# Another start for a four-layer graph network: the first graph's x before the weights, and the weight products shared out among three engines

## The chip, the cores and the metric

One Trainium2 chip, one of its cores. The metric is the device time of one execution in microseconds (us), the median over the runs. The engines are named as in the profile: PE is TensorE (matrix products), PEld its weight loads, DVE is VectorE, ACT is ScalarE, POOL is GpSimd, SP is SyncE, which here only issues DMAs. A "q" behind an engine's name is its instruction queue.

## The reference

128 independent graphs of 128 nodes with 512 features each, float32, pass four layers. Each layer is followed by `x = layernorm(x + layer(x))`.

```python
# layer 0, W1 = W2 = adj, so C - A is only the bias b
out = max over n of relu((adj @ x) + b)            # one number per node, added to its row
# layer 1: attention over the masked graph
h = x @ W;  s1 = h @ a[:512];  s2 = h @ a[512:]
e = leaky_relu(s1[:, None] + s2[None, :], 0.2) * adj
out = elu(softmax(e) @ h + beta * h)
# layer 2
out = (adj @ x) @ weight + bias
# layer 3: 8 heads of 64
q, k, v = x @ Wq + bq, x @ Wk + bk, x @ Wv + bv
out = softmax(q k^T / 8 + where(adj == 0, -1e9, 0)) v
```

## The kernel before

**Layer 1 without h.** The kernel never forms `h @ a`. It folds W into a once: `wa1 = W @ a[:512]` and `wa2 = W @ a[512:]`, two vectors of 512, each spread over all 128 partitions (`wa_bc[0]` and `wa_bc[1]`). After that s1 and s2 of a graph are row sums of `x1 * wa_bc[i]` (line 440). To build `wa_bc`, `w1_a` multiplies the four chunks of W (128x512 each) with a half of a that a DMA has spread over the partitions (`a_bc`), sums each row on the way (line 319, four instructions on DVE for each half), lays the four columns of sums on a diagonal (`wa_diag`, line 322) and lets a product with a matrix of ones spread them (line 333); line 336 copies the result out of PSUM.

**A graph's steps.** `l0` is layer 0: a product with adj^T (line 424, `psA`), its row maximum (line 427, `mx`), relu with the bias (line 431, `rl`), adding it to x (line 432), then the layer norm. Every layer norm is four engines' work: statistics on DVE (377, 379), three instructions of 128x1 on POOL (382, 384, 386: `ve`, `rstd`, `nmr`), the normalising pass on ACT (388). Then come the attention of layer 1 (`e`, `pe`, `att`), `zT` = (att x)^T, `z` = the product with W, `yT` and `y` for layer 2, `xT` (x3 turned), and for each group of four graphs q, k and v of layer 3, `sc` (scores) and `av` (weights times v).

**Sevens.** All big products but those of the first four graphs use a scheme with seven products of half-size blocks in place of eight. It needs sums and differences of blocks: of the weights, once (`weight_sums`, line 367, four instructions of 128x512 for each of the five weight matrices), and of the data, each time (`T`, line 732, four for each group; `Tz` and `Ty`, line 550). The first four graphs ("early") take `z` and `y` as whole products, and turn by TensorE instead of by DMA.

**What sets the order.** The schedule is written out by hand: all instructions stand in each engine's queue in the order in which the Python code emits them, and every engine works through its queue in order, waiting in front of each instruction until its inputs are there. The class `Plan` decides that order. It keeps an estimated clock for each engine; a step is a Python generator that yields `(engine, us, landing, rank)` before it emits, and resumes when the estimate says that the engine is free. `place` gives the TensorE steps their priorities, buffers are counted in `plan.left`, and `mark` says that something is ready. So an altered cost or mark at the beginning can alter the emitted order anywhere behind it.

**Loads.** SP's queue: adj, the two halves of `a` (each read from HBM once for each of 128 partitions, 256 KB), then x of graph 0 and graph 1, then x of each later graph when one of the two `x0` buffers is free, that is after the last use in line 440 of the graph two before. ACT's queue: W1 in four pieces, then `later_loads`: W2, Wq, Wk, the bias of layer 2, Wv, the bias of v, at times that the plan sets.

Of the kernel before, what the change touches and what calls it, by code (L numbers as in the profile page):

```python
# [9 lines left out]
F32 = mybir.dt.float32  # L10
AF = mybir.ActivationFunctionType
ALU = mybir.AluOpType
AX = mybir.AxisListType

P = 128
# [132 lines left out]
def kernel(  # L148
# [18 lines left out]
    nc = tc.nc  # L167
    ctx.enter_context(tc.manual_schedule())
    B, N, C = x.shape
    NCC = C // P  # L170
    H, HD = 8, 64
# [6 lines left out]
    sb_bufs = {  # L178
# [4 lines left out]
    }  # L183
# [9 lines left out]
    small = ctx.enter_context(tc.tile_pool(name="small", bufs=5))  # L193
    plan = Plan({**sb_bufs, **ps_bufs, **hbm_bufs, "va": NV, "w": 0})

    def ps_tile(tag, name):
        return psum.tile([P, 512], F32, tag=tag, name=name, bufs=ps_bufs[tag])

    def sb_tile(tag, shape, name):
        return sb.tile(shape, F32, tag=tag, name=name, bufs=sb_bufs[tag])  # L200

    def get(tag, shape, name):
        yield tag
        return sb_tile(tag, shape, name)
# [5 lines left out]
    def dve(us, rank=1):  # L210
        return ("DVE", us - 0.09, 0.09, rank)

    def act(us, rank=1):
        return ("ACT", us - 0.1, 0.1, rank)

    def pool(us, rank=1):
        return ("POOL", us, 0.0, rank)

    def sp(us, landing, rank=1):
        return ("SP", us, landing, rank)  # L220
# [5 lines left out]

    def load_x(b):
        x0[b] = yield from get("x0", [P, C], f"x0_{b}")
        yield sp(0.35, 2.5 if b > 1 else 5.5 + b)
        nc.sync.dma_start(out=x0[b], in_=x[b])  # L230
        plan.mark(("x0", b))

# [13 lines left out]
        nc.gpsimd.dma_start(out=t, in_=v.rearrange("(c p) -> p c", p=P))  # L246
        return t

    a_flat = a1.rearrange("f o -> (f o)")
    a_bc = [None, None]  # L250
    for i in (1, 0):
        a_bc[i] = sb_tile("xp", [P, C], f"a_bc{i}")
        nc.sync.dma_start(out=a_bc[i], in_=a_flat[i * C : (i + 1) * C].partition_broadcast(P))
        plan.left["xp"] -= 1
    w1_sb, w1_in = load_w(w1, "w1_sb")
    for c in range(NCC):
        nc.scalar.dma_start(out=w1_sb[:, c], in_=w1_in[:, c])
# [11 lines left out]

    def later_loads():  # L270

        for us, dst, src in (
            (9.5, w2_sb, w2_in), (1.0, wq_sb, wq_in), (4.0, wk_sb, wk_in), (1.0, bias2_bc, bias2_in), (4.0, wv_sb, wv_in),
            (1.0, bv_bc, bv_in),
        ):
            yield sp(0.0, us)
            if len(src.shape) < 4:
                yield act(0.16)
                nc.scalar.dma_start(out=dst, in_=src)
                continue  # L280
            yield act(0.34)
            for b in range(NQ):
                nc.scalar.dma_start(out=dst[b * Q : (b + 1) * Q], in_=src[b])
# [23 lines left out]
    wa_bc = [const.tile([P, C], F32, tag=f"wa_bc{i}", name=f"wa_bc{i}") for i in range(2)]  # L307
    plan.engine["DVE"] = 6.0

    def w1_a():  # L310

        yield sp(0.0, 6.5)
        for i in (1, 0):
            junk = yield from get("x2", [P, C], f"wa_junk{i}")
            dg = yield from get("oT", [P, NCC, P], f"wa_diag{i}")
            yield dve(3.9)
            cols = small.tile([P, NCC], F32, tag="cols", bufs=2, name=f"wa_cols{i}")
            for c in range(NCC):
                nc.vector.scalar_tensor_tensor(
                    junk, w1_sb[:, c, :], 1.0, a_bc[i], ALU.mult, ALU.mult, accum_out=cols[:, c : c + 1]  # L320
                )
            nc.vector.tensor_tensor(
                dg,
                ident.unsqueeze(1).to_broadcast([P, NCC, P]),
                cols.unsqueeze(2).to_broadcast([P, NCC, P]),
                ALU.mult,
            )
            plan.give("x2")
            plan.give("xp")
            yield "mm"  # L330
            ps = ps_tile("mm", f"ps_wa{i}")
            yield ("PE", 1.0, 0.0, 1)
            nc.tensor.matmul(ps, ones, dg.rearrange("p c n -> p (c n)"), start=True, stop=True)
            plan.give("oT")
            yield dve(0.7)
            nc.vector.tensor_copy(wa_bc[i], ps)
            plan.give("mm")
            plan.mark(("wa", i))
        yield dve(0.5)
        nc.vector.tensor_scalar(bq_s, bq_col, QS, None, ALU.mult)  # L340
        nc.vector.tensor_scalar(beta_id, ident, beta_col, None, ALU.mult)
        plan.mark("beta_id")
# [5 lines left out]
    def weight_sums(n, w):  # L348

        t = const.tile([P, 3, 2, HALF], F32, tag=f"sums_{n}", name=f"sums_{n}")  # L350
        a11, a12, a21, a22 = (w[:, 2 * c : 2 * c + 2, r * HALF : (r + 1) * HALF] for r in range(2) for c in range(2))
        sums[n] = (a11, a12, a21, a22, t[:, 0], t[:, 1], t[:, 2])
        yield sp(0.0, {"z": 0.0, "y": 0.0, "q": 44.0, "k": 52.0, "v": 84.0}[n])
        if n == "q":
            for c in range(NCC):
                yield act(0.6)
                nc.scalar.mul(w[:, c, :], w[:, c, :], QS)
        if n in "zy":
            yield ("mark", ("whole", n))
        for dst, x_, y_, op in (  # L360
            (t[:, 0], a21, a22, ALU.add),
            (t[:, 1], t[:, 0], a11, ALU.subtract),
            (a21, a11, a21, ALU.subtract),
            (t[:, 2], a12, t[:, 1], ALU.subtract),
        ):
            yield pool(1.3)
            nc.gpsimd.tensor_tensor(dst, x_, y_, op)
            yield sp(0.0, 0.7)
        plan.mark(("sums", n))


# [47 lines left out]
    def l0(b):  # L419
        s = st[b]  # L420
        x1 = sb_tile("x1", [P, C], f"x1_{b}")
        xin_b = x0.pop(b)
        ps = ps_tile("mm", f"psA_{b}")
        nc.tensor.matmul(ps, adjT, xin_b, start=True, stop=True)  # L424
        yield dve(0.69)
        mx = small.tile([P, 1], F32, tag="mx0", bufs=3, name=f"mx0_{b}")
        nc.vector.tensor_reduce(mx, ps, AX.X, ALU.max)
        plan.give("mm")
        yield act(0.95)
        rl = small.tile([P, 1], F32, tag="rl", bufs=3, name=f"rl_{b}")  # L430
        nc.scalar.activation(rl, mx, AF.Relu, bias=b0_col)
        nc.scalar.activation(xin_b, xin_b, AF.Identity, bias=rl)  # L432
        yield from layernorm(xin_b, x1, f"0_{b}")
        s["x1"] = x1
        cols = []
        for i in (1, 0):
            yield ("mark", ("wa", i))
            yield dve(0.82)
            col = small.tile([P, 1], F32, tag=f"s{i}", bufs=6, name=f"s{i}_{b}")
            nc.vector.scalar_tensor_tensor(  # L440
                xin_b, x1, 1.0, wa_bc[i], ALU.mult, ALU.mult, accum_out=col
            )
            if i == 0:
                plan.give("x0")
                if b + sb_bufs["x0"] < B:
                    plan.at(plan.end, load_x(b + sb_bufs["x0"]))
            cols.append(col)
            if i and b < EARLY:
                dg = yield from get("s2_bc", [P, P], f"diag_{b}")
                yield dve(0.3)  # L450
                nc.vector.tensor_scalar(dg, ident, col, None, ALU.mult)
                s["diag"] = dg
                plan.mark(("diag", b))
        s2, s["s1"] = cols
        if b < EARLY:
            plan.mark(("s1", b))
            return
        s2_row = yield from get("s2_row", [P, Q], f"s2_row_{b}")
        yield dve(0.2)
        nc.vector.transpose(s2_row, s2.to_broadcast([P, Q]))  # L460
        d = yield from get_hbm("s2_hbm", [NQ, Q], f"s2_hbm_{b}")
        yield sp(0.35, 3.0)
        nc.sync.dma_start(out=d, in_=s2_row.rearrange("(q r) c -> q r c", r=Q)[:, 0, :])
        plan.give("s2_row")
        s2_bc = yield from get("s2_bc", [P, P], f"s2_bc_{b}")
        yield sp(0.35, 5.0)
        nc.sync.dma_start(out=s2_bc, in_=d.rearrange("q c -> (q c)").partition_broadcast(P))
        plan.give("s2_hbm")
        yield from attention(b, s2_bc, "s2_bc")
# [746 lines left out]
    }  # L1216
    total = {name: B for name in steps}
    total.update(s2=EARLY, attT=EARLY, xT=EARLY, pT=LATE, z1=EARLY, y1=EARLY, z=7 * (B - EARLY) // 2, y=7 * (B - EARLY) // 2, avT=B - LATE, av=2 * LATE, **{n: 7 * (B // GB) for n in "qkv"})
    for b in range(sb_bufs["x0"]):
        plan.at(1.0, load_x(b))  # L1220
    plan.at(0.0, w1_a())
    plan.at(0.0, later_loads())
    for n, w in (("z", w1_sb), ("y", w2_sb), ("q", wq_sb), ("k", wk_sb), ("v", wv_sb)):
        plan.at(0.0, weight_sums(n, w))
# [32 lines left out]
```

## Time and profile before

| what | value |
|---|---|
| median of 3 runs | 2707.15 us (2698.55, 2707.15, 2709.77) |
| the profiled execution's own time | 2699.37 us |
| its span, first to last instruction | 2697.3 us |
| its mean granted TensorE clock | 0.994 |
| PE busy | 2601.1 us (96%) |
| DVE, POOL, ACT busy | 2246.2 (83%), 1822.0 (68%), 1795.9 us (67%) |
| DMA | 425.11 MB, mean 158 GB/s |

The busy shares are means over the whole span. The table of windows, the waits and the timeline, which the next part shows, tell where the 4% without TensorE work lie. In them "x4" counts instructions, the time in brackets is what the engine idled before the instruction, and "<-" names what it waited for. A float32 product shows as two matmul records. Durations come from this one execution.

### The profile page before, as it was taken

To read this page: it belongs to the slowest core of one execution; us is meant where nothing else is said; L and a number is where in the kernel's file an instruction comes from. 1 tells how busy PE (TensorE), PEld (TensorE's weight loads), DVE (VectorE), ACT (ScalarE), POOL (GpSimd) and SP (SyncE) were. 2 spreads that over 40 slices of the span, in tenths; PEclk is the share of its full clock that TensorE was granted. 3 is DMA by queue.
4 is the path that set the end of the run, shared out by engine and by line. 5 is a ranking of instruction groups with operands and counts; after the bars stand their busy time and mean duration, and the time that the engine had idled before them with its cause. 6 is when DMAs were issued, how large, how long until landed. Compare 5 with 4: busy or idle time off the path is not lost. (4 is left out here: it accounts for less than half of the span.)

```text
span 2697.3 us, 48358 instructions
## 1 busy us (share of the span) xinstructions
PE 2601.1 (96%) x15393; PEld 2207.8 (82%) x15393; DVE 2246.2 (83%) x4561; ACT 1795.9 (67%) x4847; POOL 1822.0 (68%) x2664
## 2 busy tenths in 40 slices
PE   6899999999999999999999999999999999999998
PEld 3688878888888888888888888888888888888887
DVE  7579888888888888888888888888888898889876
ACT  4566667566666676666766767676767666667655
POOL 4756667766777667667667676667776667677665
PEclk8999999999999999999999999999999999999999
DMA  5145445555444555545565445654545644455553
GB/s 132 37 122 167 149 149 163 161 187 161 155 154 147 183 164 181 152 144 167 161 186 160 150 141 192 200 165 153 155 154 170 202 148 138 149 172 174 164 176 122
DMA packets 435006, 425.11 MB, mean 158 GB/s; under 512 B 99264, under 2 KB 319552, under 8 KB 434752
## 3 DMA queue, kind: packets, MB, share of 16 engines
q1 hardware_dynamic: 431504, 416.26, 49.7%
q10 hardware_dynamic: 3120, 5.77, 0.8%
q8 instruction: 122, 2.00, 0.3%
q14 instruction: 132, 1.08, 0.1%
q0 software_dynamic: 128, 0.01, 0.0%
HBM read 218.17 MB, written 203.75 MB: 156 GB/s over the span
## 5 line engine op out<-in xcount | busy, mean ns | idle before, releaser
L388 ACT ACTIVATE x<-x,nmr,rstd 128x512 f32<-128x512 f32 x384 | 311.2, 812 | 178.1 <-POOL nmr L386 170.9
L1045 ACT ACTIVATE pr<-pr,nm 128x128 f32<-128x128 f32 x992 | 386.2, 395 | 31.1 <-DVE nm L1040 30.1
L382 POOL TENSOR_SCALAR ve<-mv 128x1 f32<-128x1 f32 x512 | 137.9, 269 | 323.7 <-DVE mv L379 250.0
L384 POOL TENSOR_TENSOR rstd<-ve,nhalf 128x1 f32<-128x1 f32 x512 | 309.8, 605 | 42.6
L377 DVE BATCH_NORM_STATS2 stats<-x 128x6 f32<-128x512 f32 x384 | 259.7, 676 | 25.7 <-ACT x L432 24.7
L440 DVE SCALAR_TENSOR_TENSOR x<-x,wa_bc 128x512 f32<-128x512 f32 x256 | 218.0, 856 | 27.3 <-ACT x L388 26.6
L922 POOL TENSOR_TENSOR st_v<-st_v,bv_bc 128x512 f32<-128x512 f32 x96 | 124.5, 1297 | 138.8 <-ACT st_v L908 137.3
L706 POOL TENSOR_TENSOR x<-x,bias_bc 128x512 f32<-128x512 f32 x128 | 173.5, 1362 | 64.0 <-PE ps_yT L713 41.5
L1128 POOL TENSOR_TENSOR x3r<-turn_o,x3r 128x512 f32<-128x512 f32 x122 | 198.3, 1625 | 20.1 <-DMA x3r<-x_hbm 10.7
L1126 POOL TENSOR_TENSOR turn_o<-turn_o,rd 128x512 f32<-128x512 f32 x122 | 140.0, 1148 | 105.8 <-DVE turn_o L407 89.9
L386 POOL TENSOR_SCALAR nmr<-mv,rstd 128x1 f32<-128x1 f32 x512 | 160.7, 314 | 52.9
L1045 ACT ACTIVATION_READ_ACCUMULATOR pr<-pr,nm 128x1 f32 x976 | 188.7, 193 | 0.0
L407 DVE STREAM_TRANSPOSE turn_pr<-turn_pr 128x1024 f32<-128x1024 f32 x122 | 150.0, 1232 | 31.2 <-DMA turn_pr<-turn_hbm_pr 31.1
L1034 DVE TENSOR_TENSOR pr<-ps_sc,mask 128x512 f32<-128x512 f32 x248 | 162.0, 675 | 14.8 <-PE ps_sc L1012 14.5
L1114 ACT COPY oT<-ps_av 128x512 f32<-128x512 f32 x122 | 132.0, 1082 | 51.9 <-PE ps_av L1102 41.6
L411 DVE STREAM_TRANSPOSE xTh<-turn_x 128x512 f32<-128x512 f32 x124 | 137.5, 1112 | 15.1 <-DMA turn_x<-turn_hbm_x 14.3
L1040 DVE TENSOR_REDUCE nm<-pr 128x8 f32<-128x1024 f32 x124 | 147.7, 1202 | 2.2 <-ACT w_sb L1045 1.9
L559 PEld LDWEIGHTS ps_zT<-attT,x 128*128 128x128 f32 x1024 | 133.3, 192 | 19.4 <-issue 5.8
L424 PE MATMUL psA<-x,adjT 128*128 128x512 f32 x256 | 135.3, 614 | 10.6 <-DMA x<-in_x_dram 9.8
L1012 PEld LDWEIGHTS ps_sc<-kTh,qTh 64*128 64x128 f32 x2048 | 121.8, 187 | 27.1 <-issue 16.0
L388 ACT ACTIVATE x3r<-x3r,nmr,rstd 128x512 f32<-128x512 f32 x122 | 98.7, 812 | 65.9 <-POOL nmr L386 58.7
L559 PE MATMUL ps_zT<-attT,x 128*128 128x128 f32 x1024 | 137.7, 278 | 4.2 <-DVE attT L411 2.3
(198 smaller groups left out, 7666.4 us busy)
## 6 DMA issues: line engine op xcount, KB each, us to landing
turn_hbm_pr<-pr SPq DMA_DIRECT2D x122, 512.0 KB
turn_pr<-turn_hbm_pr SPq DMA_DIRECT2D x122, 512.0 KB
x<-in_x_dram SPq DMA_DIRECT2D x128, 256.0 KB
x3r<-x_hbm SPq DMA_DIRECT2D x128, 256.0 KB
x_hbm<-x SPq DMA_DIRECT2D x124, 256.0 KB
turn_hbm_x<-x SPq DMA_DIRECT2D x124, 256.0 KB
turn_x<-turn_hbm_x SPq DMA_DIRECT2D x124, 256.0 KB
turn_hbm_o<-oT SPq DMA_DIRECT2D x122, 256.0 KB
```

Of the source, the lines that this page charges most:

```text
L377: nc.vector.bn_stats(stats, src if flat is None else flat)
L384: nc.gpsimd.tensor_tensor(rstd, ve, nhalf, ALU.pow)
L386: nc.gpsimd.tensor_scalar(nmr, mv[:, 0:1], rstd, -1.0, ALU.mult, ALU.mult)
L388: nc.scalar.activation(dst, src, AF.Identity, bias=nmr, scale=rstd)
L407: nc.vector.transpose(t.rearrange("p a n c -> p (a n c)"), t.rearrange("p a n c -> p (a n c)"))
L440: nc.vector.scalar_tensor_tensor(xin_b, x1, 1.0, wa_bc[i], ALU.mult, ALU.mult, accum_out=col)
L559: nc.tensor.matmul(ps[:, c * P : (c + 1) * P], s["x1"][:, c * P : (c + 1) * P], attT, start=True, stop=True)
L706: nc.gpsimd.tensor_tensor(x2, x2, bias2_bc, ALU.add)
L1034: nc.vector.tensor_tensor(pr_h[:, NCC * e : NCC * (e + 1)], pss[e].rearrange("p f (b c) -> p f b c", b=NQ), mask_bc, ALU.add)
L1040: nc.vector.tensor_reduce(nm, pr_h, AX.XY, ALU.max, negate=True)
L1045: nc.scalar.activation(pr_h[:, i], pr_h[:, i], AF.Exp, bias=nm[:, i : i + 1], accum_out=None if late else den[:, i : i + 1])
L1128: nc.gpsimd.tensor_tensor(xp_m, o.rearrange("p a n c -> p a (n c)"), xp_m, ALU.add)
```

## The change

Seven edits, all in the first part of the program.

1. `a` is loaded once, as one row on one partition (`a_row`, 4 KB), instead of twice spread over 128 partitions.
2. x of graph 0 is issued on SP right behind it, by hand. The plan is told that it is there at 6.0; x of graph 1 is now what the plan's `load_x` starts with.
3. The row is spread by TensorE: two products with a row of ones into two PSUM banks (`a_bc`). ACT copies the first half to SBUF (`a_sb`); the second is read from PSUM.
4. `w1_a` is split. The products of W1 with the second half stay four instructions on DVE, one by one as W1's pieces come. Those with the first half become four multiplications on POOL, each followed by a pass on ACT that sums the rows. Both copies of line 336 go from DVE to ACT.
5. The load of W2 waits for `rl` of graph 0. Before, it was emitted straight behind W1.
6. The weight sums of q and k go from POOL to DVE, eight instructions of 128x512. Those of z, y and v stay on POOL.
7. In `weight_sums` the plan's pause of 0.7 behind each sum is taken out.

```diff
-        yield sp(0.35, 2.5 if b > 1 else 5.5 + b)
+        yield sp(0.35, 2.5 if b > 1 else 7.0)
...
-    for i in (1, 0):
-        a_bc[i] = sb_tile("xp", [P, C], f"a_bc{i}")
-        nc.sync.dma_start(out=a_bc[i], in_=a_flat[i * C : (i + 1) * C].partition_broadcast(P))
-        plan.left["xp"] -= 1
+    a_row = sb_tile("pr", [P, H * P], "a_row")[0:1, :]
+    nc.sync.dma_start(out=a_row, in_=a1.rearrange("f o -> o f"))
+    plan.left["pr"] -= 1
+    x0[0] = sb_tile("x0", [P, C], "x0_0")
+    nc.sync.dma_start(out=x0[0], in_=x[0])
+    plan.left["x0"] -= 1
+    plan.marks["x0", 0] = 6.0
...
+        yield ("mark", ("rl", 0))
         for us, dst, src in (
-            (9.5, w2_sb, w2_in), (1.0, wq_sb, wq_in), ...
+            (0.0, w2_sb, w2_in), (1.0, wq_sb, wq_in), ...
...
+    a_bc = [ps_tile("mm", f"ps_a{i}") for i in range(2)]
+    a_sb = sb_tile("x2", [P, C], "a_sb")
...
+    for i in range(2):
+        nc.tensor.matmul(a_bc[i], ones[0:1, :], a_row[:, i * C : (i + 1) * C], start=True, stop=True)
+    nc.scalar.copy(a_sb, a_bc[0])
+
+    def w1_a_part(i, c):
+
+        prod = yield from get("x2", [P, C], f"wa_prod{i}_{c}")
+        col = wa_cols[i][:, c : c + 1]
+        if i:
+            yield dve(0.82, 0)
+            nc.vector.scalar_tensor_tensor(prod, w1_sb[:, c, :], 1.0, a_bc[1], ALU.mult, ALU.mult, accum_out=col)
+        else:
+            yield pool(1.35, 0)
+            nc.gpsimd.tensor_tensor(prod, w1_sb[:, c, :], a_sb, ALU.mult)
+            yield act(0.95)
+            nc.scalar.activation(prod, prod, AF.Identity, accum_out=col)
...
     def w1_a(i):
...
-            yield dve(0.7)
-            nc.vector.tensor_copy(wa_bc[i], ps)
+        yield act(0.6)
+        nc.scalar.copy(wa_bc[i], ps)
...
-            yield pool(1.3)
-            nc.gpsimd.tensor_tensor(dst, x_, y_, op)
-            yield sp(0.0, 0.7)
+            if n in "qk":
+                yield dve(0.72, 2)
+                nc.vector.tensor_tensor(dst, x_, y_, op)
+            else:
+                yield pool(1.3)
+                nc.gpsimd.tensor_tensor(dst, x_, y_, op)
...
         nc.scalar.activation(rl, mx, AF.Relu, bias=b0_col)
+        if b == 0:
+            plan.mark(("rl", 0))
```

In the emitted programs PE has one product more for each half of `a`, ACT seven instructions more (a copy, four summing passes, two copies from DVE), POOL four fewer (four multiplications more, eight sums fewer), DVE two more (eight sums more, four products and two copies fewer), SP one DMA fewer. The two programs stand in different order on every engine to the end: of TensorE's 7,731 products, 4,088 stand in another place in a comparison of the two lists.

More of the change, by code (lines that the diff above doesn't have):

```diff
@@ L247, in load_col @@
         return t
-    a_flat = a1.rearrange("f o -> (f o)")
-    a_bc = [None, None]
-    for i in (1, 0):
-        a_bc[i] = sb_tile("xp", [P, C], f"a_bc{i}")
-        nc.sync.dma_start(out=a_bc[i], in_=a_flat[i * C : (i + 1) * C].partition_broadcast(P))
-        plan.left["xp"] -= 1
+    a_row = sb_tile("pr", [P, H * P], "a_row")[0:1, :]
[5 more added lines that the diff above has]
+    plan.marks["x0", 0] = 6.0
     w1_sb, w1_in = load_w(w1, "w1_sb")
@@ L270, in later_loads @@
     def later_loads():
+        yield ("mark", ("rl", 0))
         for us, dst, src in (
-            (9.5, w2_sb, w2_in), (1.0, wq_sb, wq_in), (4.0, wk_sb, wk_in), (1.0, bias2_bc, bias2_in), (4.0, wv_sb, wv_in),
+            (0.0, w2_sb, w2_in), (1.0, wq_sb, wq_in), (4.0, wk_sb, wk_in), (1.0, bias2_bc, bias2_in), (4.0, wv_sb, wv_in),
             (1.0, bv_bc, bv_in),
@@ L308 @@
     plan.engine["DVE"] = 6.0
[L310 to L327, printed above, removed]
-            plan.give("x2")
[L329 to L334, printed above, removed]
-            yield dve(0.7)
-            nc.vector.tensor_copy(wa_bc[i], ps)
-            plan.give("mm")
-            plan.mark(("wa", i))
@@ new lines @@
+    a_bc = [ps_tile("mm", f"ps_a{i}") for i in range(2)]
+    a_sb = sb_tile("x2", [P, C], "a_sb")
+    wa_cols = [small.tile([P, NCC], F32, tag="cols", bufs=2, name=f"wa_cols{i}") for i in range(2)]
+    plan.left["mm"] -= 2
+    plan.left["x2"] -= 1
+    for i in range(2):
[12 more added lines that the diff above has]
+            nc.scalar.activation(prod, prod, AF.Identity, accum_out=col)
+        plan.give("x2")
+        plan.mark(("col", i, c))
@@ new lines, in w1_a @@
+    def w1_a(i):
+        cols = wa_cols[i]
+        for c in range(NCC):
+            yield ("mark", ("col", i, c))
+        if i == 0:
+            plan.give("x2")
+            plan.give("pr")
+        plan.give("mm")
+        dg = yield from get("oT", [P, NCC, P], f"wa_diag{i}")
+        yield dve(0.75, 0)
+        nc.vector.tensor_tensor(
+            dg,
+            ident.unsqueeze(1).to_broadcast([P, NCC, P]),
+            cols.unsqueeze(2).to_broadcast([P, NCC, P]),
+            ALU.mult,
+        )
+        yield "mm"
+        ps = ps_tile("mm", f"ps_wa{i}")
+        yield ("PE", 1.0, 0.0, 1)
+        nc.tensor.matmul(ps, ones, dg.rearrange("p c n -> p (c n)"), start=True, stop=True)
+        plan.give("oT")
+        yield act(0.6)
+        nc.scalar.copy(wa_bc[i], ps)
+        plan.give("mm")
+        plan.mark(("wa", i))
+        if i:
+            return
@@ L1218 @@
     total.update(s2=EARLY, attT=EARLY, xT=EARLY, pT=LATE, z1=EARLY, y1=EARLY, z=7 * (B - EARLY) // 2, y=7 * (B - EARLY) // 2, avT=B - LATE, av=2 * LATE, **{n: 7 * (B // GB) for n in "qkv"})
-    for b in range(sb_bufs["x0"]):
+    for b in range(1, sb_bufs["x0"]):
         plan.at(1.0, load_x(b))
-    plan.at(0.0, w1_a())
+    plan.at(0.0, w1_a(1))
+    plan.at(0.0, w1_a(0))
+    for c in range(NCC):
+        for i in (1, 0):
+            plan.at(6.0 + 1.2 * c, w1_a_part(i, c))
     plan.at(0.0, later_loads())
```

## The prediction

> **What bounds the kernel now.** I first read the table of windows (columns: window, its length, then busy us and instruction count of PE, PEld, DVE, ACT and POOL, granted clock, DMA share, GB/s).
>
> ```profile
> 0.00:40.00 40.00, 20.36 (x48) 9.83 (x49) 25.89 (x68) 12.82 (x25) 9.32 (x22) 0.83 0.74 192
> 40.00:60.00 20.00, 17.62 (x69) 9.98 (x68) 17.44 (x38) 12.08 (x26) 13.24 (x20) 1.00 0.11 30
> 60.00:100.00 40.00, 29.03 (x120) 18.22 (x119) 23.91 (x55) 20.98 (x45) 34.34 (x44) 0.96 0.31 61
> 100.00:135.00 35.00, 33.69 (x163) 28.91 (x164) 20.95 (x44) 18.54 (x40) 22.50 (x28) 0.95 0.08 20
> 135.00:270.00 135.00, 134.88 (x776) 115.92 (x776) 111.06 (x237) 87.31 (x240) 82.16 (x123) 1.00 0.48 145
> 270.00:1350.00 1080.00, 1050.70 (x6265) 897.71 (x6262) 916.28 (x1868) 737.97 (x2006) 742.80 (x1094) 1.00 0.52 161
> 1350.00:2430.00 1080.00, 1061.53 (x6346) 906.34 (x6345) 927.69 (x1880) 740.48 (x2018) 749.51 (x1098) 1.00 0.53 164
> ```
>
> From 135 us on TensorE is the bound. Its idle time is 29.3 us in the first 1080 us behind 270 and 18.5 in the next. Before 135 it idles 40.00-20.36 = 19.6, then 2.4, 11.0 and 1.3: 34.3 us, and that is what an edit of the start can reach. Then I read the waits of PE up to 135 us (us in total, times, longest), and ACT's largest.
>
> ```profile
> PE psA L424 <- DMA x<-in_x_dram: 7.9, 2, 6.7
> PE ps_wa L333 <- DVE wa_diag L322: 5.1, 1, 5.1
> ...
> PE ps_q_chain L888 <- POOL T L732: 6.2, 1, 6.2
> PE ps_yT L713 <- ACT x L388: 3.2, 2, 1.7
> PE ps_y L600 <- ACT yT L540: 1.6, 1, 1.6
> ...
> ACT x L388 <- POOL nmr L386: 17.7, 9, 5.1
> ```
>
> Two chains, then: x and `wa_bc` for graphs 0 and 1, and later POOL, which has every layer norm and all weight sums in its queue (34.34 of 40 us busy from 60 to 100). Last, the timeline at these places.
>
> ```profile
> 10.74 3.75 PE L424 MATMUL psA<-x,adjT 128*128 128x512 f32 x4 [6.72 <-DMA x<-in_x_dram]
> 12.82 0.69 DVE L427 TENSOR_REDUCE mx<-psA 128x1 f32<-128x512 f32 x1 [0.45 <-PE psA L424]
> ...
> 20.56 2.08 PE L333 MATMUL ps_wa<-wa_diag,ones 128*128 128x512 f32 x2 [5.11 <-DVE wa_diag L322]
> ...
> 23.04 0.81 ACT L388 ACTIVATE x<-x,nmr,rstd 128x512 f32<-128x512 f32 x1 [3.02 <-POOL nmr L386]
> ...
> 27.44 2.08 PE L424 MATMUL psA<-x,adjT 128*128 128x512 f32 x2 [1.22 <-DMA x<-in_x_dram]
> ...
> 52.72 1.26 POOL L367 TENSOR_TENSOR sums_q<-wq_sb 128x512 f32<-128x512 f32 x1
> 52.80 1.73 DVE L440 SCALAR_TENSOR_TENSOR x<-x,wa_bc 128x512 f32<-128x512 f32 x1
> ...
> 100.22 3.51 PE L888 MATMUL ps_q_chain<-T,sums_q 128*128 128x256 f32 x8 [6.23 <-POOL T L732]
> ```
>
> A product of 512 columns takes 2.08 us behind idle time, 1.02 later. The chain that ended last lies in the last 12 us and says nothing on the start.
>
> **Loads (edits 1, 2, 5).** Up to 12 us the queues moved about 3.1 MB: adj, 0.5 MB of a, two x, W1 and W2. Without the spread a and W2 it is 1.6 MB; at the DMA view's rates in the first slices of 1.5 us (0, 187, 190, 249, 353, 330 GB/s) that is there at 8 us, not 12. So x of graph 0 comes between 5 and 8 us, not at 10.7, and W1's last piece at about 8, not 10.9. W2's megabyte then lies in front of Wq, Wk and Wv on ACT's queue: at the 230 GB/s of 20 to 30 us it pushes them back 4.4 us. Wq is first used at 47.3 (line 357), so I cost this at nothing; were it not covered, those 4.4 us would fall on the q sums. Costed the same way, at nothing: the issue of W2 (0.39), in front of the second `rl`.
>
> The one row has no counterpart; the nearest rows are adj (64 KB, issued 0.73, there at 3.57) and the bias of layer 0 (0.5 KB, 5.9 us to landing). Issued at 1.2, it lands between 4.0 and 7.1. I take 4.0, as adj goes by the same queue. The Trainium skill ("DMA: Bandwidth & Descriptors", rules for kernel authors) speaks against the edit: an access pattern whose outermost dimension is smaller than 16 confines a DMA to that many of the engines. By it the row would use one of 16; no run here shows what that costs for 4 KB.
>
> **Spreading a on TensorE (edit 3)** puts two cold products in front of the first `psA`: 2 x 2.08 from 4.0 to 8.2 us. So although x is there sooner, `psA` of graph 0 runs from 8.2 to 10.3, and its maximum is taken from 10.3, 2.5 us before 12.82. With the row at 7.1 all of this is 3.1 later: the gain is gone, and 0.6 lost.
>
> **wa_bc (edit 4).** DVE keeps four products of 0.74 (from 8.2) and the two maxima; `wa_diag` of the second half ends at 13.9, against 12.4. The first half: ACT's table load 1.28 and copy 0.6 end at 8.1, POOL's four multiplications (1.3 each, as line 367) at 13.3, the passes on ACT (0.72 + 0.19 each) wait for them and stand among the two `rl` (0.29) and adding passes (0.72), and end at 16. Behind these, Wq's four issues (1.80) block ACT to 17.8. Then the copy (0.6, from DVE), and the normalising passes of graphs 0 and 1 follow at 18.4 and 19.2: ready at 19.2 and 20.0, against 20.0 and 23.85. Graph 1 gains most because its statistics no longer stand behind four products on DVE. The second copy ends at 20.6. DVE's four row sums of line 440 then end at about 20.0, 21.0, 22.0 and 23.0; the last use of x of graph 0 is the third, at 22.0 against 24.44, of graph 1 at 23.0 against 26.49. These free the two buffers for graphs 2 and 3, and PE's queue has `psA` of graph 2 in front of graph 0's `attT`: it waited to 27.44, 3.0 us behind the release. With the same 3.0 it starts at 25.0. So graph 0 moves 2.4 us, graph 1 3.5; **I take -3.0**, bounds -3.5 and +0.6.
>
> **q's and k's sums (edits 6, 7).** POOL loses 8 x 1.26 to 1.72 = 11.1 us between 52 and 72, where ACT waited up to 5.1 us for one `nmr`. DVE gains 8 x 0.69 = 5.5; it is idle for 2.5, 1.9 and 0.9 there, and three row sums at 52.8 to 57.9 that took 1.73 beside POOL's 128x512 work would take 0.68 without it (up to -3.2). So DVE is about even, and POOL's relief reaches `yT`, `y` and their waits of 3.2 + 1.6 = 4.8 us in this stretch. **I take -3.5**; bounds -4.8 and 0.
>
> A sum with both inputs in SBUF can itself meet POOL (z's sums now come early). By the row, a hit costs 1.73-0.68 = 1.05 us, eight hits 8.4. The Trainium skill's "SBUF — State Buffer" (Who interferes with whom) speaks against the move: the shared port pair is an exclusive lock held for a whole instruction, and the loser blocks fully. By that rule a hit could cost all of POOL's 1.27, and eight 10.2. POOL's new multiplications at the start meet DVE products that read PSUM; such a DVE instruction took 0.68 beside a sum of POOL at 63.4, so I cost those at nothing (4 x 1.05 if not).
>
> **Group 0's turn.** TensorE waits 6.2 us for the second `T`, and the product behind it runs cold: 3.51 for 1.89. `T` was late because ACT stood in front of it for an `s_bc` transfer (2.5 and 3.1 us idle, at 92.6 and 97.3), and because POOL put a layer norm and a `Tz` between the first and second `T`. In the new order the last `xTh` copy stands ahead of one of those ACT waits, and y's sums ahead of `T`. From the last `xT` I count ACT 0.6, `T` 1.27, `Tz` 0.72, `T` 1.27 = 3.9, against `k_first` 1.73 and a `z_chain` 0.86 on PE: 1.3 of waiting remain. Of 7.8 **I take -6.0**; bounds -7.8 and 0, as the other ACT wait stays in front of an earlier `xTh`.
>
> **The order behind.** In the two PE lists I count changes between row-tiled scores, column-tiled `av` and whole products: 265 before, 246 now. A z_chain of four takes 0.86 to its successor and 0.97 next to such a change: 19 x 0.10 = **-1.9**. The waits are dealt anew: nine stretches of 240 us from 270 to 2430 idle 8.1, 7.3, 4.8, 6.7, 5.1, 2.4, 3.9, 4.9 and 4.6, spread 1.8; over nine, and for the difference of two orders, 1.8 x 3 x 1.41 = 7.6 either way, taken as 0. The two cold products add nothing beyond the above.
>
> Sum: -3.0-3.5-6.0-1.9 = -14.4. The profiled execution, 2699.37 (span 2697.3 and 2.07 around it), would become 2685.0; it lies 7.8 below the median, so the median goes to 2707.15-14.4 = 2692.8. About 0.5% (13.5 us) is what a measurement of this kernel can tell from no change.
>
> **Rivals.** *Earlier, but not passed on.* If POOL's relief is eaten by hits on DVE and an `s_bc` wait still holds `T`, -3.0-1.9 and half of the 9.5 remain: about -9.6, 2697.5. For it: TensorE idles only 2.4 us from 40 to 60. *The row is late or its products slow*: the start gains nothing, and -11.4 gives 2695.8. *Slower: the new order waits as the worst stretch did.* From 270 to 2430 it would idle 9 x 8.12 = 73.1, not 47.8: +25.3, less about 10 at the start: 2722. It decides from 7.9 us per 240, where 47.8+10+13.5 = 71.3 is reached. Against it: only one stretch in nine is there.
>
> **How the numbers follow.** The forecast, all three start terms as taken, 0.50: faster. The two rivals short of it, 0.40 together: within 0.5%. The slower one 0.10. The best end is -3.5-4.8-7.8-1.9-7.6 = -25.6, 2681.5, and three runs differ by 11 us, so 2679; the worst end with start terms at 0.6 and the order at +7.6 is 2715. Leaving out most of the slower rival: 2679 to 2714.
>
> **What would show it.** Right: `psA` of graph 0 from about 8.2, its x before that; `psA` of graph 2 at 25; the wait for `T` under 2 us; PE idle 22 to 25 us, not 34, before 135; 45 to 50 in 270 to 2430. Wrong: the row's product after 5; `psA` of graph 2 past 27; DVE rows of line 393 at 1.7; a new PE wait of over 3 us before 135; more than 60 idle in 270 to 2430.

## The result, and the profile after

| | before | after |
|---|---|---|
| median of the runs | 2703.76 us (20 runs, 2697.72 to 2709.77) | 2711.36 us (20 runs, 2706.89 to 2721.12) |
| ratio after / before | | 1.0031, 95% interval 1.0022 to 1.0040 |
| the profiled execution, and its span | 2699.37, 2697.3 | 2717.06, 2715.3 |
| mean granted clock, PE busy | 0.994, 2601.1 | 0.991, 2612.7 |

The changed kernel is slower, by 7.6 us in the medians. The prediction said 14 us faster. The two profiled executions lie 17.7 us apart, because one is among the quicker of its kernel and the other among the slower; their difference is used below for where time lies, not for how much it is.

First the table of windows of the kernel after (same columns and windows as the prediction's, with the end of the program added).

```profile
0.00:40.00 40.00, 24.36 (x51) 10.86 (x52) 21.64 (x59) 16.81 (x36) 13.65 (x26) 0.79 0.64 173
40.00:60.00 20.00, 17.95 (x73) 10.16 (x72) 17.53 (x42) 14.24 (x30) 10.79 (x18) 1.00 0.17 47
60.00:100.00 40.00, 33.79 (x134) 22.35 (x133) 30.36 (x68) 19.80 (x44) 30.00 (x41) 0.96 0.35 70
100.00:135.00 35.00, 35.00 (x179) 30.38 (x178) 22.83 (x49) 20.56 (x44) 20.81 (x30) 1.00 0.09 23
135.00:270.00 135.00, 131.13 (x749) 112.21 (x748) 109.75 (x232) 86.23 (x238) 82.07 (x121) 0.99 0.46 144
270.00:1350.00 1080.00, 1051.77 (x6242) 896.28 (x6241) 920.53 (x1843) 729.19 (x1991) 742.09 (x1081) 1.00 0.52 162
1350.00:2430.00 1080.00, 1052.47 (x6264) 898.27 (x6263) 923.95 (x1861) 731.48 (x1999) 748.91 (x1092) 1.00 0.51 161
2430.00:2716.00 286.00, 266.26 (x1719) 232.33 (x1717) 213.14 (x412) 176.55 (x479) 174.99 (x256) 0.98 0.49 156
```

Subtract PE's busy time from each window's length. Before 135 us TensorE idles 15.6 + 2.1 + 6.2 + 0 = 23.9 us; it was 34.3. The start did become denser (3.8 of these 10.4 us are the two added products of the row, which are work and not gain). Behind it the sign turns: 3.9 idle from 135 to 270 (0.1 before), 28.2 + 27.5 = 55.8 from 270 to 2430 (47.8 before). So what was gained in the first twentieth of the program was lost again in the rest, where the change edits nothing and only the emitted order is another (the last row adds 5.0: 19.0 idle from 2430 to the end, 14.0 before).

Next the timeline of the start, at the places where the prediction named a time (start, duration, what; in brackets the idle time before and what ended it).

```profile
4.24 3.78 PE L318 MATMUL ps_a<-a_row,ones 1*128 1x512 f32 x4
...
10.06 0.69 DVE L455 TENSOR_REDUCE mx<-psA 128x1 f32<-128x512 f32 x1 [0.70 <-PE psA L452]
...
11.12 0.39 ACTq L281 DMA_DIRECT2D w_sb<-in_L_gnn_weight_dram  x1
...
19.13 0.68 DVE L470 SCALAR_TENSOR_TENSOR x<-x,wa_bc 128x512 f32<-128x512 f32 x1
...
19.85 1.14 SPq L230 DMA_DIRECT2D x<-in_x_dram  x2
...
27.02 2.04 PE L452 MATMUL psA<-x,adjT 128*128 128x512 f32 x2 [6.14 <-DMA x<-in_x_dram]
...
97.65 1.99 PE L918 MATMUL ps_q_chain<-T,sums_q 128*128 128x256 f32 x8
```

The row's products and graph 0's maximum come at 4.2 and 10.06, where the prediction put them (4.0, 10.3). The last use of graph 0's x ends at 19.82 against 24.44: 4.6 us earlier, more than the 2.4 worked out. At 19.85 SP asks for graph 2's x. Yet its product starts at 27.02, only 0.4 us earlier than before: the load is now used 7.2 us after it is asked for, where it took 3.0. The wait of 6.2 us for `T` in front of `ps_q_chain` is gone from TensorE's line at 97.65, and the product there runs in 1.99 instead of 3.51.

Last, the largest waits of PE from 135 to 2640 us (total, times, longest), the kernel before first, then the one after.

```profile
PE ps_y_pair L581 <- DVE x L760: 8.4, 9, 2.5
...
PE ps_y_chain L581 <- ACT sty L748: 1.8, 3, 0.9
...
PE ps_q_chain L888 <- ACT st_q L913: 0.9, 3, 0.4
```

```profile
PE ps_y_chain L611 <- ACT sty L778: 12.9, 16, 1.7
PE ps_q_chain L918 <- ACT st_q L943: 8.5, 7, 2.6
```

`sty` and `st_q` are copies, on ACT, of a finished half product out of its PSUM bank; TensorE waits for them when its next product needs that bank. Summed over all rows of this view, PE waits 48.0 us before (for ACT 5.6) and 63.3 after (for ACT 26.2). For DVE it waits less, 28.2 before and 18.7 after.

### The profile page after: what moved, and what is told of

It reads as the page before. It is cut to its first block, busy times and chain, and to the rows that moved or that the text cites. A ratio compares the mean times of both kernels' runs of the same rounds, so it can differ in the third digit from the quotient of the medians.

```text
span 2715.3 us, 48323 instructions
## 1 busy us (share of the span) xinstructions
PE 2612.7 (96%) x15397; PEld 2212.8 (81%) x15397; DVE 2259.7 (83%) x4559; ACT 1794.8 (66%) x4858; POOL 1823.3 (67%) x2660
## 4 chain that ended last, share of the span: by engine, by line
PE 43%; DVE 14%; POOL 13%; issue 5%; DMA 4%; ACT 4%; SPq 0%; POOLq 0%; DVEq 0%; ACTq 0%
PE ps_z_chain L611 5%; PE ps_v_chain L918 5%; PE ps_k_chain L918 3%; PE ps_q_chain L918 3%; PE ps_y_chain L611 3%; PE ps_z_pair L611 2%; POOL rstd L412 2%; PE ps_zT L589 2%; PE ps_v_pair L918 2%; DMA turn_pr<-turn_hbm_pr 2%; PE ps_av L1132 2%; PE ps_sc L1042 2%; PE ps_q_pair L918 2%; PE ps_k_pair L918 2%; DVE stats L405 2%
## 5 line engine op out<-in xcount | busy, mean ns | idle before, releaser
L743 PEld LDWEIGHTS ps_yT<-adjT,x 128*128 128x128 f32 x1024 | 129.2, 193 | 26.5 <-ACT x L416 12.6
```

## The experiments

The theory after the result had two halves: the start gains 8 to 10 us, and the new order behind it loses more than that. Its rivals: the start's own edits cost something that only shows later (W2 late, weight sums on DVE in POOL's way), with the order no better or worse than any other; or the load of graph 2's x, held up by W2, is the whole loss.

To hold the order fixed, the kernels below do not run the planner (except where said) but emit a recorded list of its steps:

```diff
-        while any(nxt[name] < total[name] for name in steps):
-            ... the planner picks the next step
+        for name in ORDER.split():
+            if name not in self.gens:
+                step, b = name.rsplit(".", 1)
+                self.gens[name] = steps[step][-1](int(b))
+            next(self.gens[name], None)
```

Every experiment was compared with runs of the kernel before on the same chip. Line numbers in the profiles of kernels with a list are some 205 to 215 higher.

**1 and 2. Start and order crossed.** `ORDER` is the first 540 or so steps of one kernel, up to about 100 us, and the remainder of the other's list. At that point the two lists hold the same steps but for some twenty, apart from those that the edits themselves change.

Start of after, order of before:

> The whole start of the changed kernel (all seven edits), and from about TensorE's 170th product on the instruction order of the kernel before, to the last instruction. Theory O (the start gains, the new order behind it costs): TensorE idles 24 us instead of 34 before 135 us, 3.8 of that are the two added products, so about 6 us faster than before: ratio 0.997 to 0.999, and the idle time from 270 to 2430 us falls back to about 48 us with one cold stretch. Rival S (the start itself is slower than it looks, for example by its changed transfers): as slow as the changed kernel, ratio 1.002 to 1.004.

Measured: 2695.33 against 2703.87 us, ratio 0.9970 (0.9959 to 0.9981).

Start of before, order of after:

> The start of the kernel before, and from about TensorE's 160th product on the instruction order of the changed kernel. Theory O: the order costs what it costs in the changed kernel, without the gain of the start: 10 to 16 us slower than before, ratio 1.004 to 1.006, idle time from 270 to 2430 us about 56 us with four or five cold stretches. Rival S: the order is worth nothing, ratio 0.999 to 1.001.

Measured: 2723.61 against 2703.87, ratio 1.0073 (1.0061 to 1.0086), more than expected. With the kernels themselves this makes a square:

| | order of before behind | order of after behind |
|---|---|---|
| start of before | 1 | 1.0073 |
| start of after | 0.9970 | 1.0031 |

Read along the columns, the start gains 0.0030 and 0.0042, 8 to 11 us. Read along the rows, the order loses 0.0073 and 0.0061, 20 and 16 us. The waits of PE from 135 to 2640 us follow the order and not the start. First crossing 1, then crossing 2:

```profile
PE ps_y_chain L821 <- ACT sty L988: 2.5, 4, 1.0
...
PE ps_q_chain L1128 <- ACT st_q L1153: 1.9, 3, 0.8
```

```profile
PE ps_y_chain L791 <- ACT sty L958: 12.0, 15, 1.8
...
PE ps_q_chain L1098 <- ACT st_q L1123: 7.8, 6, 2.7
```

In total 49.3 us (for ACT 7.1) and 65.7 (27.1). Both halves of the theory hold. The cold stretches that were expected beside them do not simply follow the order: in slices of 20 us between 135 and 2640 there are two with a granted clock under 0.985 in either crossing, where one and four or five were expected. What crossing 2 loses is mostly idle time of PE: 115.4 us over its span against 96.2 in the kernel before.

*How the order makes that wait.* The timeline of the kernel after shows one of the sixteen:

```profile
454.84 1.03 PE L611 MATMUL ps_y_chain<-sums_y,Ty 128*128 128x256 f32 x4
455.80 1.09 PE L1132 MATMUL ps_av<-turn_pr,va 128*64 128x128 f32 x16
456.21 0.81 ACT L416 ACTIVATE x<-x,nmr,rstd 128x512 f32<-128x512 f32 x1 [1.20 <-POOL nmr L414]
456.93 0.45 ACT L943 ACTIVATE st_q<-ps_q_chain,bq_s 128x256 f32<-128x256 f32 x1
457.51 0.81 ACT L416 ACTIVATE x<-x,nmr,rstd 128x512 f32<-128x512 f32 x1
458.23 0.35 ACT L778 COPY sty<-ps_y_chain 128x256 f32<-128x256 f32 x1
...
458.63 1.75 PE L611 MATMUL ps_y_chain<-sums_y,yT 128*128 128x256 f32 x4 [1.74 <-ACT sty L778]
```

The product of 454.84 is done at 455.9, but its copy stands in ACT's queue behind two normalising passes and an `st_q`, and the first of these waits for a layer norm on POOL. It starts at 458.23, and TensorE, with one short step between, stands for 1.74 us. I counted how many `sty` copies start over 1.5 us behind the end of their product, of 186: 11 before, 14 in crossing 1, but 29 after and 27 in crossing 2. That is a reading of the traces; no run moved those copies alone, and kernel 9 below is slower without them.

**3 and 4. W2 back behind W1**, each other step in its place: 3 with the order of after, 4 with that of before.

```diff
+    nc.scalar.dma_start(out=w2_sb, in_=w2_in)      # straight behind W1's four pieces
...
-                nc.scalar.dma_start(out=dst, in_=src)
+                if dst is not w2_sb:
+                    nc.scalar.dma_start(out=dst, in_=src)
```

> The changed kernel in its own order, with one edit undone: W2 is loaded straight behind W1 again. In the changed kernel x of graph 2, asked for at 19.9 us, landed at 27.0, behind W2, Wq and half of Wk. Theory D (the load of x stands in line behind all that was asked for before it, on whichever queue): without W2's 1 MB in front, 4 us less, so the third product psA starts at 23 to 24 us and graph 0's z 3 to 4 us earlier than at 33.3; x of graph 0 comes later, at 8 to 10 us. The total falls by 0 to 4 us against the changed kernel, ratio to before 1.001 to 1.003. Rival: the transfer is slow for another reason (the rate of SP's own queue), psA still starts at 27 and nothing moves.

> The first hybrid (start of the changed kernel, order of the kernel before behind it) with W2 loaded straight behind W1. Theories O and D together: 2 to 4 us less than the first hybrid, 6 to 10 us faster than before, ratio 0.996 to 0.998. If only O holds, the same as the first hybrid; if neither, ratio 1.002 to 1.004.

Measured: 3 ran 2717.66 against 2703.87, ratio 1.0057 (1.0043 to 1.0070), which is slower than after with W2 late, and than the 1.001 to 1.003 expected. 4 ran 2692.67 us, ratio 0.9965 (0.9952 to 0.9977), which the intervals do not part from crossing 1. The timeline of kernel 3:

```profile
25.92 2.05 PE L665 MATMUL psA<-x,adjT 128*128 128x512 f32 x2 [5.02 <-DMA x<-in_x_dram]
```

So W2's deferral is not what made the kernel slower, and moving it buys graph 2's product 1.1 us, not the 3 to 4 expected: a miss. The rest of Wq and Wk still moves at that time. Why kernel 3 is slower than after, with its product of graph 2 earlier, stays open; its waits from 135 to 2640 are 67.3 us against 63.3.

**5. Wq's and Wk's issue as well.** On top of 4 the loads are placed again: Wq stays at 13.3 us, Wk moves behind the bias (from 17.7 to 26.5 us in the traces), Wv follows it.

```diff
-            (0.0, w2_sb, w2_in), (1.0, wq_sb, wq_in), (4.0, wk_sb, wk_in), (1.0, bias2_bc, bias2_in), ...
+            [], [(wq_sb, wq_in)], [], [(bias2_bc, bias2_in)], [(wk_sb, wk_in)], [(wv_sb, wv_in), (bv_bc, bv_in)],
```

> As the hybrid with W2 early (start of the changed kernel, order of the kernel before behind it), and the loads spread anew: Wq is issued where Wk was (17.7 us) less one place, that is at 13.3 with nothing in the place of W2, the bias of layer 2 where it was, Wk where Wv was (about 29 us), Wv and its bias last. In the hybrid with W2 early x of graph 2, asked for at 19.9, still landed only at 25.9, with Wk asked for from 17.7 on. Theory D (a load stands in line behind all that was asked for before it): with Wk out of the way it lands 2.5 to 3.5 us behind the request, psA of graph 2 starts at 22.5 to 23.5, graph 0's z 3 us earlier, at 29 us; the total another 2 to 3 us lower, ratio 0.995 to 0.997. Rival: a load of 256 KB takes 6 us at that point whatever stands before it; psA stays at 26 and the ratio at 0.9965.

Measured: 2689.40 against 2704.57, ratio 0.9948 (0.9935 to 0.9960): faster than both kernels, by 15 us than before, and a little below the range expected. Its timeline:

```profile
20.05 1.14 SPq L440 DMA_DIRECT2D x<-in_x_dram  x2
...
23.38 2.05 PE L664 MATMUL psA<-x,adjT 128*128 128x512 f32 x2 [2.31 <-DMA x<-in_x_dram]
...
26.53 1.77 ACTq L490 DMA_DIRECT2D wk_sb<-in_L_gnn_Wk_dram  x4
```

Asked for at nearly the same time, graph 2's x is used 3.3 us later instead of 7.2 in after and 6.1 in 4, because Wk is only asked for at 26.5. The table of windows shows the queues while the load is under way, in before, after and 5 (the last columns are the share of DMA time and GB/s):

```profile
24.00:28.00 4.00, 1.77 (x5) 1.12 (x5) 2.90 (x11) 0.86 (x3) 0.00 (x0) 0.50 0.96 241
```

```profile
20.00:27.00 7.00, 0.80 (x2) 0.52 (x3) 2.12 (x9) 1.54 (x6) 0.00 (x0) 0.50 1.05 258
```

```profile
20.00:24.00 4.00, 1.41 (x3) 1.00 (x4) 2.32 (x11) 1.64 (x6) 0.00 (x0) 1.00 0.61 195
```

In after the 16 DMA engines are full for those 7 us (share 1.05) and every other engine is nearly idle; in 5 the share is 0.61. But full engines alone do not delay the load: in the kernel before the share is 0.96, and the load took 3.0. What differs is how much stood in front of it. The DMA packets of the traces tell it: behind the request of graph 2's x no packet of SP's queue starts for 1.0 us in before, 4.1 in after, 3.7 in 4 and 1.0 in 5, and in that time ACT's queue moves 0.23, 0.93, 0.83 and 0 MB. From its first packet to its last the load itself then takes 1.5 to 1.8 us in all four. So the load waited for what ACT's queue had been asked for before; moving Wk out of its way is shown to end that wait.

**6 and 7. The weight sums of q and k.** 6 is the kernel before, its list of steps, with edit 6 alone; 7 is crossing 1 with edit 6 undone.

```diff
-            nc.gpsimd.tensor_tensor(dst, x_, y_, op)                                  # 6: in before
+            (nc.vector if n in "qk" else nc.gpsimd).tensor_tensor(dst, x_, y_, op)
...
-                nc.vector.tensor_tensor(dst, x_, y_, op)                              # 7: in crossing 1, for q and k
+                nc.gpsimd.tensor_tensor(dst, x_, y_, op)
```

> The kernel before in its own order, with edit 6 alone: the eight weight sums of q and k on VectorE, at the same places of the order. The first hybrid gained 8 us by its start. Theory P (most of that is POOL's relief): PE's waits for yT, y and T between 45 and 135 us fall from 11 to about 4, total 5 to 7 us below before, ratio 0.9975 to 0.998. Rival W (it comes from the earlier x and W1's split, and VectorE only takes over the lateness): ratio 0.9995 to 1.001.

> The first hybrid (start of the changed kernel, order of the kernel before behind it) with edit 6 undone: q's and k's sums on GpSimd, at the places that the changed kernel gives them. Theory P: most of the gain is gone, ratio 0.9990 to 1.0005, with waits for T or yT of 5 us and more back before 135 us. Rival W: it keeps the gain, 0.997 to 0.998.

Measured: 6 ran 2704.41 against 2704.24, ratio 1.0000 (0.9991 to 1.0009), which also says that emitting a recorded list costs nothing of itself. 7 ran 2697.66, ratio 0.9979 (0.9970 to 0.9988), which overlaps crossing 1. The move by itself brings nothing, and the start keeps most of its gain without it. The table of windows of 6 shows that POOL was relieved, 27.80 us busy where it had 34.34, and PE's waits show that it did not help:

```profile
60.00:100.00 40.00, 31.63 (x124) 20.56 (x122) 27.38 (x62) 21.02 (x44) 27.80 (x38) 0.93 0.33 64
```

```profile
PE ps_q_chain L1098 <- POOL T L942: 4.9, 1, 4.9
PE ps_yT L923 <- ACT x L598: 3.3, 2, 2.1
PE ps_y L810 <- ACT yT L750: 1.6, 1, 1.6
```

The waits for `yT` and `y`, which the prediction wanted to shorten, are 3.3 and 1.6: 3.2 and 1.6 before. In 6 the wait for `T` also stays (4.9), and its timeline shows where it hangs; the kernel after stands behind it:

```profile
97.31 0.40 ACT L694 ACTIVATE e<-s_bc,s 128x128 f32<-128x128 f32 x1 [3.31 <-DMA s_bc<-s_hbm]
97.61 0.56 ACT L750 COPY zT<-ps_zT 128x512 f32<-128x512 f32 x1
98.26 0.72 POOL L760 TENSOR_TENSOR Tz<-zT 128x256 f32<-128x256 f32 x1 [2.23 <-ACT zT L750]
98.94 1.26 POOL L942 TENSOR_TENSOR T<-xTh,T 128x512 f32<-128x512 f32 x1
```

```profile
93.03 0.59 ACT L570 COPY zT<-ps_zT 128x512 f32<-128x512 f32 x1 [2.15 <-PE ps_zT L589]
93.69 0.73 POOL L580 TENSOR_TENSOR Tz<-zT 128x256 f32<-128x256 f32 x1 [0.77 <-ACT zT L570]
96.28 1.32 POOL L762 TENSOR_TENSOR T<-xTh,T 128x512 f32<-128x512 f32 x1
```

The second `T` stands on POOL behind a `Tz`, whose `zT` copy stands on ACT behind an `s_bc` wait. In the kernel after, and in 7, where the wait for `T` is gone without the move, that copy comes first.

**8 to 12. Is the order of after bad, or that of before good?** A constant of the planner, the time that a step's result takes to reach the next engine, is altered by a hundredth or two. The work stays the same; the planner decides anew.

```diff
-HOP = 0.35
+HOP = 0.36      # 8: before    9: before, 0.37    10: after    11: before, 0.33    12: after, 0.34
```

> The kernel before with nothing changed but one constant of its planner (the assumed hop between engines, 0.36 for 0.35 us). It computes and loads the same; from the 75th product on the order differs, 4,589 of 7,731 products in another place. Theory L (any new order deals the waits anew, by several us either way): off by 5 to 20 us, ratio 0.995 to 1.008, more likely slower, since the order of the kernel before is one that was kept. Rival (what costs time in the changed kernel is particular to its edits): within 4 us, ratio 0.9985 to 1.0015.

> The same with 0.37: 4,221 products in another place. Theory L: again off by 5 to 20 us, and by another amount than with 0.36. Rival: within 4 us.

> The changed kernel with the same constant at 0.36; its order is the changed kernel's to the 570th product (some 210 us), 3,546 of 7,733 products are elsewhere behind. Theory L: another total than the changed kernel's 1.003, anywhere from 0.994 to 1.010, with the start to 135 us as in the changed kernel. Rival (particular to the edits): 1.002 to 1.005 again.

> The kernel before with the planner's constant at 0.33. Two such neighbours (0.36, 0.37) were 10 and 16 us slower. Theory K (the order of the kernel before is a kept one, better than a neighbour drawn blindly): slower again, ratio 1.002 to 1.008. Rival (the two were chance, orders lie on both sides): 0.995 to 1.001.

> The changed kernel with the planner's constant at 0.34; at 0.35 its ratio is 1.003, at 0.36 it was 1.0057. Theory K: its start gains 8 us over the neighbours of the kernel before (1.003 to 1.006) and that is all, so 1.000 to 1.006. Rival: an order as good as that of the kernel before, 0.997 or less.

| HOP | before's code | after's code |
|---|---|---|
| 0.33 | 2722.48, 1.0065 (1.0051 to 1.0079) | |
| 0.34 | | 2713.62, 1.0034 (1.0021 to 1.0047) |
| 0.35 | 1 | 1.0031 |
| 0.36 | 2714.73, 1.0034 (1.0022 to 1.0046) | 2721.31, 1.0057 (1.0042 to 1.0072) |
| 0.37 | 2720.39, 1.0057 (1.0043 to 1.0071) | |

All three neighbours of the kernel before are slower than it, by 0.34% to 0.65%. The three orders of after are slower by 0.31% to 0.57%. Nothing parts the two sets of neighbours but, at most, the start's gain. The order of before is the exception, and every re-dealing that was run loses it. With the neighbours the waits are others, again from PE's view, kernels 8, 11 and 9:

```profile
PE ps_y_chain L581 <- ACT sty L748: 13.1, 12, 1.4
PE ps_zT L559 <- DVE attT L411: 9.3, 12, 2.4
```

```profile
PE ps_zT L559 <- DVE attT L411: 10.3, 10, 2.2
PE ps_y_chain L581 <- ACT sty L748: 7.0, 9, 1.5
```

```profile
PE ps_y_chain L581 <- POOL Ty L550: 10.1, 10, 1.9
```

In 8 and 11 `sty` is late too, and `attT` besides, so that wait is no property of this change. In 9 it is not: TensorE waits 1.8 us for `sty`, as before, and 12 copies start late, against 11, yet the kernel is 16 us slower. There it waits for `Ty` (4.9 before), in all 54.9 us against 48.0. So late copies are one way in which an order can be worse, and not the only one.

## Why the prediction was wrong

**The step that failed** is "The waits are dealt anew ... 7.6 either way, taken as 0". It measured +16 us (order of after against order of before, on the start of after) and +20 (on the start of before), outside the 7.6. Two things were wrong in it. The width was taken from nine stretches of one order, which share that order's quality, so it says how stretches differ and not how orders do. And zero as the centre supposes that the order in hand is an average draw. The five neighbours of experiments 8 to 12 say that it is not: each lies above it. A centre of +14, the mean of before's three neighbours (1.0052), would have turned the sum of -14.4 to about zero. The slower rival named the right part, the order's waits, and priced it at 2722; it was given 0.10 because "only one stretch in nine is there". Its size was not right either: it wanted 73.1 us idle from 270 to 2430, and 55.8 came.

**Why its trace check did not decide.** PE idles 55.8 us from 270 to 2430, between the "45 to 50" for right and the "more than 60" for wrong. The idle time of 270 to 2430 is 8.0 of the loss only; 3.8 more lie between 135 and 270, 5.0 behind 2430, and PE's busy time grew by 11.6, of which the two new products are 3.8. The rest of that growth is clock: in slices of 20 us with a granted clock under 0.985 the kernel after loses some 9 us in five places between 135 and 2640, the kernel before 1.8 in one. How much of that belongs to the order is open: with the same order behind, crossing 2 has two such places and kernel 3 four.

**Start of the first layer, -3.0.** Row, products and maximum came as worked out, and the four row sums of graphs 0 and 1 ended 2.1 to 2.8 us earlier than worked out. The rule of the Trainium skill that the prediction set against the one row ("DMA: Bandwidth & Descriptors", rules for kernel authors) cost nothing here: the row did go undivided, as a single packet of 4 KB in the trace, but at 3.12 and in 0.16 us, and its product stands at 4.24 and waits for nothing. What was wrong is "With the same 3.0 it starts at 25.0": it started at 27.02, as the sign for wrong ("past 27") had it. The 3.0 was the load's time with 0.23 MB in front of it on ACT's queue; when after asks for this x, 4.6 us earlier, 0.93 MB of weights still stand there. The prediction pushed Wq back by 4.4 us and asked only who needs Wq, not what else shares the way. The Trainium skill's page "DMA: Bandwidth & Descriptors", section "Issuing engines are not separate DMA queues", says that loads asked for by different engines end on the same 16 engines and interleave there. That they share the engines fits the share of 1.05; interleaving does not show at this place, where SP's first packet comes 4.1 us behind its request and the packets of ACT's queue go on until then. Experiment 5 undoes this collision: the product comes 3.6 us earlier than in after (1.1 of it by W2's place, the rest by Wk's), and the ratio goes from 0.9965 in 4 to 0.9948, with intervals that still overlap a little.

**q's and k's sums, -3.5.** Measured 0 (1.0000, 0.9991 to 1.0009). The waits for `yT` and `y` did not shorten with POOL free for 6.5 us more. The cost side was about right: of the eight sums one took 1.75 and one 1.04 on DVE, six 0.64 to 0.68. The Trainium skill's "SBUF — State Buffer" (Who interferes with whom) lets the loser stand for the holder's whole instruction; the worst here is 1.07 over the usual 0.68. That sum began 0.07 behind one of POOL's of 1.27, so a hit costs about what the rule says, but only one of the eight was a full one.

**Group 0's `T`, -6.0.** The wait went, as said, but not by the reason given for the last `xTh` copy: in 6 that copy (92.78) stands ahead of the `s_bc` wait, and the wait for `T` is still 4.9. It hung on the `zT` copy in front of `Tz`. Nor is it a gain of its own in the end time: in after, other waits on the way grew (`yT` for x 6.3 us from 45 to 135, before 3.2). For the whole start the crossings give -8 to -11 us, where the terms named for it are 12.5 together; PE's idle time before 135, 23.9, lies inside the 22 to 25 predicted.

**Mode changes, -1.9.** No run shows it. The order with 19 fewer changes is the slower one.

**What stays open.** What makes the order of before better than all five neighbours, and whether moving the late copies alone would restore it in after; how that order came to be chosen, which no run shows; what parts kernel 3 from after; and whether edit 6 is worth anything on the new start (0.9970 with it, 0.9979 without).

## What to carry to other kernels

Where a planner emits the schedule, an edit at its beginning is two changes, the edit and a new order, and they should be measured apart by replaying the recorded order. The order in hand can be better than its neighbours, and a re-dealt one then has to be expected worse and not equal: here the three neighbours of before lose 0.34% to 0.65%, the order of after 0.61% to 0.73%. (That it is better because it was once kept for its time is a guess; no run shows it.) A load that is put off still has to be moved some time, so ask which small, urgent load it will then stand in front of.

## What the runs showed of the hardware

- A load of 256 KB asked for on SP's queue was used 7.2 us later while W2, Wq and Wk (asked for on ACT's queue before it) were moving, 3.3 us later when Wk was held back. A queue of its own gave it no way ahead: its first packet came 4.1 us behind the request, after 0.93 MB of ACT's, and 1.0 us behind it with none in front.
- A single wait of about 2 us in an otherwise dense stretch can have a second price. In the kernel after, a wait of 1.99 at 206.1 is followed by a `ps_y_chain` of 1.81 instead of 1.03 and a `ps_q_chain` of 2.94 instead of 1.89: 1.8 us lost on top. It is not the rule: of the eleven waits of PE of 1.7 us and more between 135 and 2640 in the two profiled executions, six are followed by 4 us with a granted clock of 0.57 to 0.65, and five, one of 2.73 among them, by the full clock.

```profile
206.10 1.81 PE L611 MATMUL ps_y_chain<-sums_y,Ty 128*128 128x256 f32 x4 [1.99 <-POOL Ty L580]
207.71 2.94 PE L918 MATMUL ps_q_chain<-xTh,sums_q 128*128 128x256 f32 x8
```
